# The order of TensorE written into the source, and weights loaded where the first graph needs them: a four-layer graph network

## The chip, the cores and the metric

The kernel runs on one core of one Trainium2 chip, as one launch. The metric is the device time of that launch in microseconds. A core has five engines that run side by side, each with its own instruction queue: TensorE (PE in the profile, its weight loads as PEld), VectorE (DVE), ScalarE (ACT), GpSimd (POOL) and SyncE (SP), which issues the kernel's transfers. They wait for each other through semaphores. Matrix products land in banks of PSUM, all other tiles lie in SBUF.

## The reference

32 graphs, each with 512 nodes of 256 features and a 512 x 512 integer adjacency matrix, go through four layers that all use the same adjacency. After each layer stands a residual sum and a layer norm without parameters.

```python
def reference(x, adj, ...):                      # x: (32, 512, 256), adj: (32, 512, 512)
    # layer 0: four heads of 64; weight by edge type, leaky relu, masked softmax, bias,
    # relu, + h, then a layer norm for each head
    x = _layernorm(x + _L0_gnn_ref(x, adj, W, a_src, a_dst, bias, ln_gamma, ln_beta))
    # layer 1: one head; h = x W, e = relu(f_src + f_dst), masked softmax, att h, elu
    x = _layernorm(x + _L1_gnn_ref(x, adj, W, a))
    # layer 2: transformer block: qkv, eight heads of 32 with the mask
    # adj or adj transposed or the diagonal, Wo, layer norm,
    # feed forward 256 -> 1024 -> 256 with relu, layer norm
    x = _layernorm(x + _L2_gnn_ref(x, adj, Wqkv, bqkv, Wo, bo, ln1, W1, b1, W2, b2, ln2))
    # layer 3: one head; leaky relu (0.2), masked softmax, att h
    x = _layernorm(x + _L3_gnn_ref(x, adj, W, a))
    return x
```

## The kernel before

A graph stays on the chip from its load to its store. All products with 512 nodes are made in blocks of 128 rows (`R` = 4) and 128 features (`K` = 2).

The steps of a graph, with the names under which their tiles stand in the profile:

- *load* and *masks*: `adjt` and `adj` come in halves of 256 rows into one buffer (tag `adj`), SyncE issues them (L320 is the first of them). ScalarE makes `at`, the transposed adjacency in bytes (L340). VectorE makes `a2`, the symmetric mask (`tensor_max`, L347). In the rows of `ADDED`, `a2` is turned into 0 for an edge and -2^127 for none.
- *layer 0*: `h0p` (L297) is x times the weights and eight more columns for the two attention vectors. For each head, `along` transposes one column into a row on all partitions (`gp`, L311; copied by ScalarE to `gb`, L315), VectorE makes the masked numerators `pt` (`kept`, L360), and sixteen products of 65 columns (`o0`, L386; 32 instructions in the profile) fill a bank. After the four heads stand a layer norm for each head (`head_layernorm`) and one over the row (`layernorm`: `bn` and `rs` on VectorE, a power on GpSimd at L243, `y` on ScalarE at L248).
- *layer 1*: transposes `xt1p` (L285), `h1p` (L297), `gp1`, four rows of `o1` (`attend`, L415) with a reciprocal (L440), relu and exp behind each.
- *qkv*: transposes `xt2p`, products `qkp` (L458) and `vp` (L484). q and k are split in a high and a low part (`hi`, `lo`) that 64 transfers on SyncE's queue rearrange into `qk`.
- *attention*: four head pairs. For each block of rows a score product `s` (L506), in the rows of `ADDED` a second product that adds the mask (L514, identity times `a2`), the exponential (L515, ScalarE), and in the other rows a multiplication with the mask (L518, VectorE). Then sixteen instructions `cp` (L526), the product with V.
- *projection*: transposes `ctp` and `ct` (their copies by ScalarE at L277), `wop` (L567).
- *feed forward*: transposes `ytp`, products `f1p` (L590) and `f2p` (L604). The layer norms around it are folded in part into the weights (`bf1p`, L199, and the scaling of `wf1` at L208) and the vectors.
- *layer 3*: like layer 1: `xt3p`, `h3p`, `gp3`, `o3` (L415).

PSUM is split by stage: the steps up to layer 1 take two banks (tag `mma`), qkv to projection four (`mmb`), the rest two (`mmc`).

**What sets the order.** The kernel is written graph by graph, but every step carries a priority, and a list scheduler orders the instructions of each engine by it:

```python
PERIOD = 457
RANK = {"load": 120, "layer 0": -480, "layer 1": -330, "qkv": 0, ...}
    def step(name):
        tc.trace_state.cur_priority = first + PERIOD * b + RANK[name]
```

So four graphs are in work at a time: while graph g is in layers 0 and 1, graph g-1 is in attention, g-2 in projection and feed forward, g-3 in layer 3. Within this the scheduler places instructions one by one. The `cp` products of a head pair are kept together by a raised priority and an added dependency ("one go").

**The weights.** Ahead of the first graph, SyncE issues the loads of all weights and vectors (L123 to L193), among them short columns taken out of vectors with a stride (`bqk`, `bvc`, `bf1`, L134 to L138, and `lnc`, L193), and broadcasts of a vector to all partitions (`bcast`, L94). Then come the set-up computations (L162 to L208): the attention vectors multiplied into columns of the weights (products at L170, reductions at L162 and L176), a bias through `wo` (`bop`) and one through `wf1` (`bf1p`). The first graph's loads are issued after these.

Of the kernel before, what the change touches and what calls it, by code (L numbers as in the profile page):

```python
# [24 lines left out]
ADDED = (1, 3)  # L25
# [3 lines left out]

PERIOD = 457  # L30
RANK = {
    "load": 120,
    "layer 0": -480,
    "layer 1": -330,
    "qkv": 0,
    "attention": 80,
    "projection": 480,
    "feed forward": 510,
    "layer 3": 550,
}  # L40
ALL = mybir.DependencyInfo(mybir.DependencyClass.Sync, mybir.DependencyReason.DATA)
# [22 lines left out]
def fast_path(ctx: ExitStack, tc: tile.TileContext, a: dict, out: bass.AP, bad: bass.AP):  # L64
# [24 lines left out]
    const = ctx.enter_context(tc.tile_pool(name="const", bufs=1))  # L89

    def bcast(src: bass.AP, name: str, n: int, pool=None):

        t = (pool or const).tile([P, n], F32, name=name)
        nc.sync.dma_start(t, bass.AP(tensor=src.tensor, offset=src.offset, ap=[[0, P], [1, n]]))  # L94
        return t
# [19 lines left out]
    def load_w(src: bass.AP, name: str, cols: int, extra: int = 0):  # L115
        kk = src.shape[0] // P
        t = const.tile([P, kk, cols + extra], F32, name=name)
        nc.sync.dma_start(t[:, :, :cols], src.rearrange("(k p) c -> p k c", p=P))
        return t

    w0 = const.tile([P, K, D + 2 * H], F32, name="w0")
    for k in range(K):
        nc.sync.dma_start(  # L123
            w0[:, k, :D].rearrange("p (h e) -> p h e", h=H),
            a["w0"][:, k * P : (k + 1) * P, :].rearrange("h p e -> p h e"),
        )
    w1g = load_w(a["w1g"], "w1g", D, 2)
    w3g = load_w(a["w3gt"], "w3g", D, 2)
    wqkv = load_w(a["wqkvt"], "wqkv", 3 * D)
    wo = load_w(a["wot"], "wo", D)  # L130
    wf1 = load_w(a["w1t"], "wf1", F)
    wf2 = load_w(a["w2t"], "wf2", D)
    bqk = const.tile([P, 2 * K], F32, name="bqk")
    nc.sync.dma_start(bqk, a["bqkv"][: 2 * D].rearrange("(c p) -> p c", p=P))  # L134
    bvc = const.tile([P, K], F32, name="bvc")
    nc.sync.dma_start(bvc, a["bqkv"][2 * D : 3 * D].rearrange("(c p) -> p c", p=P))
    bf1 = const.tile([P, NF], F32, name="bf1")
    nc.sync.dma_start(bf1, a["b1"].rearrange("(c p) -> p c", p=P))  # L138
    bo = bcast(a["bo"], "bo_b", D)
    lnb2 = bcast(a["b2"], "b2_b", D)  # L140
    bias0 = bcast(a["bias0"], "bias0_b", D)
    gam0 = bcast(a["gam0"], "gam0_b", D)
    bet0 = bcast(a["bet0"], "bet0_b", D)
    ln1g = bcast(a["ln1g"], "ln1g_b", D)
    ln2g = bcast(a["ln2g"], "ln2g_b", D)
    ln2b = bcast(a["ln2b"], "ln2b_b", D)

    with (
        tc.tile_pool(name="setup", bufs=1) as setup,
        tc.tile_pool(name="setup_ps", bufs=1, space=bass.MemoryType.PSUM) as setup_ps,  # L150
    ):

        for s, name in enumerate(("a0s", "a0d")):
            ab = setup.tile([P, H, HO], F32, name=name + "_b")
            src = a[name]
            nc.sync.dma_start(
                ab,
                bass.AP(tensor=src.tensor, offset=src.offset, ap=[[0, P], [T * HO, H], [1, HO]]),
            )
            for k in range(K):  # L160
                prod = setup.tile([P, H, HO], F32, name="prod")
                nc.vector.tensor_mul(prod, w0[:, k, :D].rearrange("p (h e) -> p h e", h=H), ab)  # L162
                nc.vector.tensor_reduce(
                    w0[:, k, D + s * H : D + (s + 1) * H], prod, axis=X, op=ALU.add
                )
        for w, name in ((w1g, "a1"), (w3g, "a3")):
            ab = bcast(a[name], name + "_b", 2 * D, setup)
            for s in range(2):
                prod1 = setup.tile([P, K, D], F32, name="prod1")
                nc.vector.tensor_mul(  # L170
                    prod1,
                    w[:, :, :D],
                    ab[:, s * D : (s + 1) * D].unsqueeze(1).to_broadcast([P, K, D]),
                )
                u = setup.tile([P, K], F32, name="u")
                nc.vector.tensor_reduce(u, prod1, axis=X, op=ALU.add)  # L176
                for k in range(K):
                    nc.vector.tensor_copy(w[:, k, D + s : D + s + 1], u[:, k : k + 1])

        p = setup_ps.tile([P, 512], F32, name="bop")  # L180
        for k in range(K):
# [6 lines left out]
            )  # L188
        nc.vector.tensor_add(bo, bo, p[:, :D])

        lnc = setup.tile([P, K, 2], F32, name="lnc")
        for i, name in enumerate(("ln1g", "ln1b")):
            nc.sync.dma_start(lnc[:, :, i], a[name].rearrange("(k p) -> p k", p=P))  # L193
        ln1b = bcast(a["ln1b"], "ln1b_b", D, setup)
        nc.vector.tensor_add(lnb2, lnb2, ln1b)
        p = setup_ps.tile([P, NF, 1], F32, name="bf1p")
        for f in range(NF):
            for k in range(K):
                nc.tensor.matmul(  # L199
                    p[:, f, :],  # L200
# [1116 lines left out]
```

## Time and profile before

| | us |
|---|---|
| time, median of 3 runs (4004.65 to 4009.49) | 4009.25 |
| the profiled execution's own time | 4009.25 |
| its span | 4007.5 |
| TensorE busy (96%) | 3837.6 |
| VectorE busy (63%) | 2509.2 |
| ScalarE busy (50%) | 1986.3 |
| GpSimd busy (8%) | 315.4 |

The span runs from the first instruction to the last. A busy share is the sum of an engine's instructions over the span. The profile names a group by line, engine, operation and tile (output and inputs, without buffer numbers). "L386 ... o<-hv,pt" is the line of layer 0's head products. A wait is listed with the engine that released it. A matrix product with 32-bit inputs shows as two instructions.

### The profile page before, as it was taken

How to read it: one execution, taken by the hardware profiler on the slowest of the kernel's cores; microseconds unless marked ns; L12 is line 12 of the kernel's file. 1: busy time of each engine (PE TensorE's matmuls, PEld its weight loads, DVE VectorE, ACT ScalarE, POOL GpSimd, SP SyncE). 2: the span in 40 equal slices, each digit the busy share in tenths (PEclk: the TensorE clock that was granted, in tenths of full speed). 3: DMA queues.
4: the chain of work that ended last, by engine and by line, in shares of the span. 5: the costliest groups of instructions: out<-in, count | busy, mean ns of one | idle time of the engine just before them, and what ended most of it. 6: DMA issues, size and time to landing. Idle time of an engine off the chain costs nothing.

```text
span 4007.5 us, 53877 instructions
## 1 busy us (share of the span) xinstructions
PE 3837.6 (96%) x19494; PEld 2817.2 (70%) x19494; DVE 2509.2 (63%) x5444; ACT 1986.3 (50%) x4257; POOL 315.4 (8%) x266
## 2 busy tenths in 40 slices
PE   4899999999999999999999999999999999999996
PEld 4567777777777777767777777777777777777654
DVE  4566666676666667666667666667666666666643
ACT  1345555455455455455545555545555545555532
POOL 0000000000000000000000000000000000000000
PEclk7899999999999999999999999999999999999998
DMA  3222222222222222222222122222222222222110
GB/s 106 74 69 56 61 64 64 79 74 59 61 60 64 79 79 59 60 61 65 74 80 69 54 61 66 70 79 69 56 61 63 69 79 69 59 62 65 48 48 12
DMA packets 184367, 261.22 MB, mean 65 GB/s; under 512 B 41120, under 2 KB 76832, under 8 KB 184096
## 3 DMA queue, kind: packets, MB, share of 16 engines
q1 hardware_dynamic: 184096, 257.71, 23.1%
q8 instruction: 157, 2.57, 0.3%
q14 instruction: 114, 0.93, 0.1%
HBM read 106.57 MB, written 16.78 MB: 31 GB/s over the span
## 4 chain that ended last, share of the span: by engine, by line
PE 77%; DVE 12%; ACT 6%; POOL 3%; issue 1%; SPq 0%; DMA 0%; POOLq 0%; ACTq 0%; DVEq 0%
PE f1p L590 11%; PE o L386 11%; PE f2p L604 10%; PE cp L526 9%; PE o L415 6%; PE qkp L458 6%; PE s L506 5%; ACT y L248 3%; PE h1p L297 3%; PE wop L567 3%; PE vp L484 3%; DVE pt L360 3%; POOL rs L243 3%; PE gp L311 2%; PE s L514 2%; DVE bn L239 2%
## 5 line engine op out<-in xcount | busy, mean ns | idle before, releaser
L515 ACT ACTIVATE pr<-s 128x512 f32<-128x512 f32 x1024 | 575.8, 606 | 330.0 <-PE s L514 185.1
L518 DVE TENSOR_TENSOR pr<-pr,a 128x1024 f32<-128x1024 f32 x256 | 309.2, 1217 | 510.1 <-ACT pr L515 510.1
L386 PEld LDWEIGHTS o<-hv,pt 128*128 128x128 f32 x4096 | 542.5, 196 | 67.4 <-DVE pt L360 30.6
L360 DVE SCALAR_TENSOR_TENSOR pt<-gb,ex,at 128x512 f32<-128x512 f32 x768 | 537.1, 742 | 83.7 <-ACT gb L315 83.5
L604 PE MATMUL f2p<-wf,ft 128*128 128x256 f32 x2048 | 575.4, 391 | 6.5 <-ACT ft L599 6.2
L248 ACT ACTIVATE y<-y,rs 128x256 f32<-128x256 f32 x768 | 405.0, 591 | 327.3 <-DVE rs L244 297.2
L590 PE MATMUL f1p<-yt,wf 128*128 128x256 f32 x2048 | 557.0, 381 | 0.5 <-ACT yt L277 0.5
L386 PE MATMUL o<-hv,pt 128*128 128x65 f32 x4096 | 543.4, 273 | 11.9 <-DVE pt L360 11.9
L506 PE MATMUL s<-qk 128*128 128x512 f32 x1024 | 508.4, 538 | 6.8 <-ACT pr L515 4.7
L415 PE MATMUL o<-h,pt 128*128 128x257 f32 x2048 | 503.9, 384 | 8.0 <-DVE pt L360 4.4
L526 PE MATMUL cp<-pr,v 128*64 128x512 f32 x2048 | 470.6, 602 | 3.6 <-ACT pr L515 3.6
L604 PEld LDWEIGHTS f2p<-wf,ft 128*128 128x128 f32 x2048 | 363.9, 191 | 136.3 <-issue 48.7
L415 PEld LDWEIGHTS o<-h,pt 128*128 128x128 f32 x2048 | 379.9, 190 | 111.3 <-issue 29.3
L590 PEld LDWEIGHTS f1p<-yt,wf 128*128 128x128 f32 x2048 | 371.5, 191 | 71.3 <-ACT yt L277 1.1
L243 POOL TENSOR_TENSOR rs<-rs,mhalf 128x4 f32<-128x4 f32 x192 | 216.4, 1127 | 2346.5 <-DVE rs L242 2298.8
L599 ACT ACTIVATE ft<-f1p,bf 128x256 f32<-128x256 f32 x512 | 218.9, 472 | 321.1 <-PE f1p L590 319.4
L526 PEld LDWEIGHTS cp<-pr,v 128*64 128x64 f32 x2048 | 136.6, 137 | 267.4 <-issue 211.1
L239 DVE BATCH_NORM_STATS2 bn<-y 128x6 f32<-128x256 f32 x768 | 296.5, 408 | 1.6
L458 PE MATMUL qkp<-xt,wqkv 128*128 128x512 f32 x512 | 245.1, 608 | 4.2 <-ACT xt L277 4.2
L506 PEld LDWEIGHTS s<-qk 128*128 128x128 f32 x1024 | 192.5, 191 | 70.1 <-issue 23.8
L315 ACT COPY gb<-gp 128x512 f32<-128x512 f32 x192 | 112.3, 585 | 194.9 <-PE gp L311 193.7
L514 PE MATMUL s<-a,identb 128*128 128x512 bf16 x512 | 196.6, 384 | 0.0
(134 smaller groups left out, 4678.7 us busy)
## 6 DMA issues: line engine op xcount, KB each, us to landing
qk<-hi SPq DMA_DIRECT2D x1024, 64.0 KB, 2.0
qk<-lo SPq DMA_DIRECT2D x1024, 64.0 KB, 2.0
adjt<-in_adjt SPq DMA_DIRECT2D x64, 512.0 KB, 3.4
adj<-in_adj SPq DMA_DIRECT2D x64, 512.0 KB, 3.6
xt<-in_xt SPq DMA_DIRECT2D x32, 512.0 KB, 3.4
x<-in_x SPq DMA_DIRECT2D x32, 512.0 KB, 4.6
out<-y SPq DMA_DIRECT2D x32, 512.0 KB, 2.9
wf<-in_w1t SPq DMA_DIRECT2D x1, 1024.0 KB, 9.6
```

The costliest lines, as they stand in the source:

```text
L239: nc.vector.bn_stats(st[:, r, :], y[:, r, :])
L243: nc.gpsimd.tensor_tensor(rs[:, 1, :], rs[:, 0, :], mhalf[:, :R], op=ALU.pow)
L248: nc.scalar.activation(y[:, r, :], y[:, r, :], AF.Identity, bias=rs[:, 2, r : r + 1], scale=rs[:, 1, r : r + 1],)
L360: nc.vector.scalar_tensor_tensor(t, g, f, edges, op0=ALU.max, op1=ALU.mult)
L386: nc.tensor.matmul(o[:, r, :], pt[j][:, r * P : (r + 1) * P], hv[:, j, hh, :], start=j == 0, stop=j == R - 1,)
L415: nc.tensor.matmul(p[:, : D + 1], pt[j][:, r * P : (r + 1) * P], h[:, j, : D + 1], start=j == 0, stop=j == R - 1,)
L458: nc.tensor.matmul(p, wqkv[:, k, (s * K + c) * P : (s * K + c + 1) * P], xt[:, k, :], start=k == 0, stop=k == K - 1,)
L506: nc.tensor.matmul(s, qk[hp][:, 1, i, j * P : (j + 1) * P], qk[hp][:, 0, i, :], start=True, stop=j not in ADDED,)
L515: last = nc.scalar.activation(t[:, i, :], s, AF.Exp, scale=QSCALE)
L526: m = nc.tensor.matmul(cp[i * 2 * DH : (i + 1) * 2 * DH, :], v[:, j, first : first + 2 * DH], pr[j][:, i, :], start=j == 0, stop=j == R - 1,)
L590: nc.tensor.matmul(p[:, f, :], wf1[:, k, (ff + f) * P : (ff + f + 1) * P], yt[:, k, r * P : (r + 2) * P], start=k == 0, stop=k == K - 1,)
L604: nc.tensor.matmul(acc[:, i, :], ft[:, f, i * P : (i + 1) * P], wf2[:, ff + f, :], start=ff + f == 0 and i == 0, stop=ff + f == NF - 1 and ...
```

## The change

TensorE's order is taken from the scheduler and written out. Each step is now a generator that yields before each of its units (the transposes into one bank, one block of rows of a product, one head pair's `cp` and so on), and `PLACES` gives each unit a place on a common scale. Graph b's units stand at `PERIOD * b + place`, and the units of all graphs are merged by that number; within a unit TensorE's instructions stand as written. The other engines' instructions are still ordered by the scheduler. The raised priority and the added dependency of `cp` go.

The loads of the weights, and the computations on them, move into the steps: when graph 0 comes to a step, that step's weights are asked for first. The first layer's weights and vectors reach the chip already joined (`w0t`, `a0`), and the short columns come as one tile `cols` in one transfer. The `bop` and `bf1p` products stand among TensorE's units of graphs 0 and 1.

The rows that take the mask by addition are 2 and 3 instead of 1 and 3. `a2` becomes two tiles, `a2m` for rows 0 and 1 in bytes and `a2a` for rows 2 and 3 in bf16, and one instruction replaces two. `xt0`, the input of layer 0's projection, has a buffer of its own.

```diff
-ADDED = (1, 3)
+ADDED = (2, 3)
...
-PERIOD = 457
-RANK = {
-    "load": 120,
-    "layer 0": -480,
-    "layer 1": -330,
-    "qkv": 0,
-    "attention": 80,
-    "projection": 480,
-    "feed forward": 510,
-    "layer 3": 550,
+PERIOD = 1205
+PLACES = {
+    "edges": [-490],
+    "x": [-197],
+    "layer 0": [
+        2, 11, 56, 83, 172, 302, 302, 302, 302, 302, 405, 405, 405, 405, 435, 533, 545, 545, 545,
+        553, 586, 586, 674, 674,
+    ],
+    "layer 1": [846, 871, 896, 920, 944, 949, 969, 1091, 1117, 1174, 1193],
+    "qkv": [1452, 1452, 1532, 1538, 1567, 1667, 1704, 1704, 1718, 1782],
+    "attention": [
+        1787, 1890, 1909, 1909, 1926, 1926, 1926, 1933, 1988, 1988, 2036, 2071, 2079, 2134, 2167,
+        2209, 2246, 2269, 2294, 2318,
+    ],
+    "projection": [2399, 2404, 2408, 2446, 2496, 2496, 2527, 2581, 2635, 2649],
+    "feed forward": [
+        2859, 2873, 2946, 2977, 2977, 2990, 3026, 3114, 3136, 3166, 3185, 3224, 3250, 3291, 3320,
+        3368, 3426, 3471,
+    ],
+    "layer 3": [3670, 3670, 3679, 3706, 3706, 3711, 3725, 3837, 3837, 3837, 3856],
 }
+STAGES = {"edges": "a", "x": "a", "layer 0": "a", "layer 1": "a", "feed forward": "c", "layer 3": "c"}
...
+    def paced(b, name, units):
+
+        i = 0
+        while True:
+            stage[0] = STAGES.get(name, "b")
+            try:
+                next(units)
+            except StopIteration as end:
+                return end.value
+            yield PERIOD * b + PLACES[name][i]
+            i += 1
...
-    for k in range(K):
-        nc.sync.dma_start(
-            w0[:, k, :D].rearrange("p (h e) -> p h e", h=H),
-            a["w0"][:, k * P : (k + 1) * P, :].rearrange("h p e -> p h e"),
-        )
-    w1g = load_w(a["w1g"], "w1g", D, 2)
-    w3g = load_w(a["w3gt"], "w3g", D, 2)
...
-    bqk = const.tile([P, 2 * K], F32, name="bqk")
-    nc.sync.dma_start(bqk, a["bqkv"][: 2 * D].rearrange("(c p) -> p c", p=P))
-    bvc = const.tile([P, K], F32, name="bvc")
-    nc.sync.dma_start(bvc, a["bqkv"][2 * D : 3 * D].rearrange("(c p) -> p c", p=P))
-    bf1 = const.tile([P, NF], F32, name="bf1")
-    nc.sync.dma_start(bf1, a["b1"].rearrange("(c p) -> p c", p=P))
...
+    cols = const.tile([P, 5 * K + NF], F32, name="cols")
...
+    def weights0():
+        load_w(w0, "w0t")
+        ab = part("a0")
+        bcast(ab, "a0")
+        bcast(bias0, "bias0")
...
+    def weights13(w, name, vectors):
+        load_w(w, name)
+        ab = part(vectors)
+        bcast(ab, vectors)
...
+    def weights2():
+
+
+        load_w(wo, "wot")
+        bcast(bo, "bo")
+        bcast(ln2b, "ln2b")
+        p = bank("bop")
...
+    def weights_ff():
+
+        load_w(wf1, "w1t")
+        load_w(wf2, "w2t")
+        bcast(ln1g, "ln1g")
+        bcast(lnb2, "b2")
+        bcast(ln2g, "ln2g")
+        ln1b = part("ln1b")[:, :D]
+        bcast(ln1b, "ln1b")
...
-        a2 = sb.tile([P, R, N], BF16, tag="a2", name="a2", bufs=2)
+        a2 = [
+            sb.tile([P, R // 2, N], dtype, tag=name, name=name, bufs=2)
+            for dtype, name in ((U8, "a2m"), (BF16, "a2a"))
+        ]
...
-        for r in ADDED:
-            nc.vector.tensor_scalar(
-                a2[:, r, :], a2[:, r, :], 0.0, SHUT, op0=ALU.is_equal, op1=ALU.mult
-            )
+        nc.vector.tensor_scalar(a2[1], a2[1], 0.0, SHUT, op0=ALU.is_equal, op1=ALU.mult)
...
-            gb = along(ex[:, 0, hh, :].unsqueeze(2), "gb0")
+            gb = yield from along(ex[:, 0, hh, :].unsqueeze(2), "gb0")
             pt = [kept("pt0", gb, at[:, j, :], ex[:, 1, hh, j : j + 1]) for j in range(R)]
             p = bank("o0")
             o = p[:, : R * HC].rearrange("p (r c) -> p r c", r=R)
             for r in range(R):
+                yield
...
-                    last = nc.scalar.activation(t[:, i, :], s, AF.Exp, scale=QSCALE)
+                        nc.tensor.matmul(s, identb, a2[1][:, j % 2, :], start=False, stop=True)
+                    nc.scalar.activation(t[:, i, :], s, AF.Exp, scale=QSCALE)
                 if j not in ADDED:
-                    edges = a2[:, j, :].unsqueeze(1).to_broadcast([P, 2, N])
-                    last = nc.vector.tensor_mul(t, t, edges)
+                    edges = a2[0][:, j, :].unsqueeze(1).to_broadcast([P, 2, N])
+                    nc.vector.tensor_mul(t, t, edges)
                 pr.append(t)
 
+            yield
...
+            yield
             cp = bank("cp")
-            with tc.high_priority(offset=4000):
-                for j in range(R):
-                    for i in range(2):
-                        first = (2 * hp + i) * VC
-                        m = nc.tensor.matmul(
-                            cp[i * 2 * DH : (i + 1) * 2 * DH, :],
-                            v[:, j, first : first + 2 * DH],
-                            pr[j][:, i, :],
-                            start=j == 0,
-                            stop=j == R - 1,
-                        )
-                        if j == 0 and i == 0:
-                            tc.add_manual_dep(m.ins, last.ins.name, ALL, reason="one go")
+            for j in range(R):
+                for i in range(2):
+                    first = (2 * hp + i) * VC
...
-    first = tc.trace_state.cur_priority - min(RANK.values())
-
-    def step(name):
-        tc.trace_state.cur_priority = first + PERIOD * b + RANK[name]
-
-    for b in range(B):
...
+    def load_all(b):
+        if b == 0:
+            weights0()
+        at_a2 = masks(b, *load(b))
+        yield
+        return at_a2
...
+    def layer1_all(b, x, at, rd):
+        if b == 0:
+            weights13(w1g, "w1g", "a1")
+        return (yield from layer1(x, at, rd))
...
+    def graph(b):
+        yield PERIOD * b + PLACES["edges"][0]
...
+        at, a2 = yield from paced(b, "edges", load_all(b))
+        xt, x = yield from paced(b, "x", load_x(b))
+        x = yield from paced(b, "layer 0", layer0_all(b, x, xt, at, rds[0]))
...
+        x = yield from paced(b, "layer 3", layer3_all(b, x, at, rds[3]))
...
+    with tc.manual_schedule(engines={mybir.EngineType.PE}):
+        for _ in heapq.merge(*(graph(b) for b in range(B))):
+            pass
```

## The prediction

> **What bounds the kernel now.** I read the page first, for the share of each engine and the forty slices; then the windows by stage, the waits of PE in the steady part, and the chain in order of time through the head and the first graph.
>
> The page:
>
> ```profile
> PE 3837.6 (96%) x19494; PEld 2817.2 (70%) x19494; DVE 2509.2 (63%) x5444; ACT 1986.3 (50%) x4257; POOL 315.4 (8%) x266
> PE   4899999999999999999999999999999999999996
> PEclk7899999999999999999999999999999999999998
> ```
>
> TensorE is busy for 96% of the span, and every slice but the first two and the last is full. The windows (columns: length, busy time of each engine, granted clock, DMA share, GB/s):
>
> ```profile
> 0.00:44.00 44.00, 9.06 (x36) 8.08 (x36) 11.78 (x30) 0.00 (x0) 2.76 (x10) 1.00 0.53 153
> 44.00:87.00 43.00, 36.55 (x160) 33.50 (x160) 19.98 (x36) 11.46 (x23) 0.00 (x0) 0.63 0.20 67
> 87.00:104.00 17.00, 0.05 (x1) 0.05 (x1) 11.67 (x21) 4.46 (x10) 3.93 (x2) 0.50 0.30 93
> 128.00:280.00 152.00, 135.58 (x687) 92.65 (x688) 93.39 (x163) 63.45 (x134) 9.37 (x6) 0.93 0.26 67
> 400.00:3590.00 3190.00, 3151.08 (x16217) 2319.31 (x16216) 2074.94 (x4524) 1656.83 (x3556) 261.04 (x214) 1.00 0.24 66
> 3925.00:4007.50 82.50, 52.11 (x198) 38.86 (x198) 21.49 (x57) 18.27 (x42) 3.02 (x3) 0.81 0.04 14
> ```
>
> From 400 to 3590, TensorE idles 39 of 3190 us, 1.2%, at full clock. A graph takes 119.5 us there (a head pair's product with V starts at 1003.74 and again at 1123.26). So an order can give at most 1.5 us a graph, unless it does worse. The rest lies in the first 280 us and in the last 80. PE's waits between 400 and 3590, the three largest (total, times, longest, us):
>
> ```profile
> PE wop L567 <- ACT ct L277: 13.7, 27, 0.5
> PE xt3p L285 <- ACT y L248: 11.6, 27, 0.4
> PE o L386 <- DVE pt L360: 6.6, 27, 0.2
> ```
>
> The chain through the head and graph 0 (start, length, what):
>
> ```profile
> 6.73 5.05 SPq L136
> 12.74 3.08 SPq L94
> 17.29 5.72 DMA bet_b<-in_bet
> 23.46 5.95 DMA lnc<-in_ln1b
> 29.45 7.00 PE bf1p L199 x32
> 40.61 4.78 DMA adjt<-in_adjt
> 55.67 13.30 PE o L386 x60
> 103.30 0.61 ACT y L248
> ```
>
> SyncE issues all weights one after another, the set-up of L199 to L208 follows the last, and only then does graph 0's load (L320) go out. The first projection (h0p) starts at 44.42. Then head outputs in a row, then a layer norm with TensorE empty from 86.1 to 103.95.
>
> **The change part by part.** The profiled execution's own time is 4009.25 (span 4007.5 and 1.75 around it), which is also the median of the runs shown.
>
> *Head.* Graph 0's step now asks first for w0, the a0 vectors and bias0, then adjt, xt and x; everything else comes behind. The first h0p needs w0 with its reduced columns. The a0 broadcast goes out second, at 1.25 (row of the second issue of L123), and the 256 KB a_b row lands in 7.0; two products of 0.69 (L170) and four small reductions of 0.42 (L162) follow: 1.25 + 7.0 + 1.38 + 1.68 = 11.3. That is 33.1 less than 44.42. Bounds from the head's own landings: 3.2 (b_b) makes it 36.9, 11.8 (w2t) makes it 28.3. I take 7.0 as the same size and shape. The first half of adjt and xt are asked for by about 4 (half a microsecond an issue, L118) and land 4.0 and 3.9 after issue in the head's rows, by 8: hidden. So is the second half of adjt, if it waits only for its buffer: the first is read by 11 (1.28 and 1.15, L340), a load of 4.8 and two more copies end by 18.5, and the first pt comes at about 19.
>
> *Graph 0's layer 0.* Before, TensorE sees the edge row of the next head (gp, L311) among the head outputs. In the new order gp of head h+1 stands behind all sixteen o0 of head h, so three heads run in series: gp 0.87, gap 0.2, its copy gb 0.59 (L315), gap 0.1, four masked rows pt 2.73 (0.76 each less overlap with the matmuls, L360), gap 0.1, and the last 26 of the matmuls that still follow, at 13.30/60 = 0.222 each, 5.76. Sum 10.35, against (86.06 - 54.35)/4 = 7.9 now. Three times 2.4: +7.3.
>
> The granted clock in that stretch bears on this:
>
> ```profile
> 55.00:110.00 55.00, 27.68 (x126) 27.09 (x126) 0.51 0.21 68
> ```
>
> That row is L386 alone: 13.30 us of unbroken 65-column matmuls and still half clock, so I take half clock for the heads after the change as well.
>
> The Trainium skill (TensorE: Matmul & The Clock Gate, Part 1) says otherwise: the gate opens after about 3.4 us of sustained activity and shuts after an idle window of that length. By the page the unbroken o0 would have run at full speed, and a head of graph 0 would take about 7.5 us, an estimate from that page, with a sum lower by some 11 us. The page also speaks against this change: it puts gaps of about 4 us into graph 0, where TensorE waits for gb and pt, and each would shut the gate. The row disagrees with the first and cannot show the second.
>
> *Work put between.* Weights of layer 1 are prepared on VectorE when graph 0 comes to layer 1, and graph 1's masks come in as well, both into the queue of graph 0's layer norm, whose chain is bare (87 to 104): two tensor_max of 1.205 (L347), two products 0.69, one reduction 0.68: +4.5. Bounds 0, and 7.9 with four products and four reductions.
>
> *bop and bf1p.* The 32 single-column matmuls (7.00, L199) and bop (2.08) leave the head, where the DMA queue would now hide them, and stand in TensorE's order in graphs 0 and 1. At full clock half of 9.08, and a share 135.58/152 = 0.89 of the time there is TensorE's: +4.0. Bounds 0 and 9.1.
>
> Head to 280 us: -33.1 + 7.3 + 4.5 + 4.0 = -17.3.
>
> *Steady part.* The order of units is nearly the present one, but whole units now stand together. Between the last ct transpose and wop stand 3.0 us of TensorE's work instead of none; between f2p and xt3p 16.5 instead of 15.2; between an edge row gp of layer 0 and its o0 at least 5.2 instead of 2.2 (each the sum of the trace's durations of what lies between). These exceed what has to be hidden (ACT's ct copy 0.5 late, y 0.4 late, pt 0.2 late), so the three waits go: 13.7/27 + 11.6/27 + 6.6/27 = 1.18 a graph. What is next: gp3 now follows the last h3p at once, where 0.66 of other work stood. The copy h (0.36), the small exp (0.21) and semaphores make 0.70, bare. I take 0.66; bounds 0 and 1.0. The three last o1 of layer 1 stand behind the last product with V of the attention (before, nine of its sixteen matmuls came first), and then h0p of the next graph takes the same two banks of stage "a": a wait for rd, relu and exp of o1 (0.59 each, L248's kind). The nearest row is the idle time before o1 and o3 now (o L415, 8.0 over 32 graphs): 0.25 a graph, a third of it, 0.08, for the last three o1. The far end is 1.9, the rival below. I take 0.3, near the row. So -1.18 + 0.66 + 0.3 = -0.22, for 29 graphs (280 to 3740 at 119.5): -6.4.
>
> Taking the mask additively in rows 2 and 3 instead of 1 and 3, one SHUT instruction instead of two and the split mask tile: equal counts on TensorE, less than 0.1 us on VectorE, which has 37% free. Nothing. If that cover went, it would be 0.1 a graph.
>
> SyncE: fewer issues in the head, none moved past a steady copy; its queue carries the same 64 copies a graph. The late weights all go out within its first 33 issues, ahead of the first of those copies. Nothing.
>
> *Drain.* The last two wop units stand behind three o3 of graph 30, work that TensorE has to do anyhow, but the last feed forward then starts later: +1 (0 to 5.2, the three o3: 24 instructions at 0.216 from start to start).
>
> Sum: 4009.25 - 17.3 - 6.4 + 1 = 3986.6.
>
> **The rivals.**
> (A) The waits go and nothing new comes. Head and graph 0 as above, -17.3; steady -1.18 x 29 = -34.2: 4009.25 - 17.3 - 34.2 + 1 = 3959. For it: covers of 3 to 16 us are all larger than the chains they hide. Against: bare h3p to gp3.
> (B) Slower: VectorE becomes late at o1. The window behind the last head pair:
>
> ```profile
> 1040.80:1070.90 30.10, 28.91 (x148) 23.28 (x148) 24.47 (x70) 16.43 (x41) 2.02 (x2) 1.00 0.10 36
> ```
>
> VectorE is busy for 81% of it. It works through ln2g, the sum with x and the next bn of the feed forward, and the reciprocal of o1 (L440), at 1045.36, comes 4.5 us after the product with V has ended. The new order wants that bank again 3.5 us after, and the relu and exp take 0.84 more: 4.5 + 0.84 - 3.5 = 1.9 of wait a graph. In place of my 0.3 this is -1.18 + 0.66 + 1.9 = +1.4 a graph, x 29 = +40: 4009.25 - 17.3 + 40 + 1 = 4033. It decides from 16.3/29 = 0.56 net loss a graph on, and it is slower by over 0.2% from 0.84 on. For it: today the scheduler can move TensorE to another ready unit; a fixed order waits for the engine that is late. Against: today this lateness costs almost nothing, 8.0 in all at o L415.
> (C) The change does not do what it says: the weights still queue in front (w1g and wqkv go out ahead of the second adjt half, whose buffer must be read first), the norm of graph 0 stretches, and steady waits are only exchanged. At its bounds the head then gives 28.3 - 7.3 - 7.9 - 9.1 = 4, so 4006 with the drain; steady -0.2 to +0.35 a graph (x 29: -6 to +10) makes it 4001 to 4017, taken as no change.
>
> **How the numbers follow.** Forecast 0.38 at 3987; (A) 0.25; (B) 0.27; (C) 0.10. The forecast's own bounds: up by gp3 at 1.0 (+10), the landing at 11.8 (+5) and the drain (+4), 4006; down by gp3 at 0 and the turn at 0.08 (-0.88 x 29 = -25), which is all but (A). The low end 3950 is (A) less 3.8 (landing at 3.2) and 4.0 (bf1p hidden). The high end 4030 cuts off the upper half of (B), 0.14, and a little of (A) falls below. A measurement of this kernel can tell about 0.2%, 8 us. Forecast and (A) are faster by more: 0.63; (C) is within: 0.10; (B) slower: 0.27.
>
> **What would show it.** In the profile after: the first h0p at 11 (9.5 to 16); gaps of about 4 us between the o0 of graph 0's heads, at clock 0.5 in 20 to 65; xt1p of graph 0 about 25 us earlier than 103.95. The waits wop on ct and xt3p on y gone, and one new of gp3 on h3's exp, 0.6 to 0.7 times some 30. The distance between rows of the same head pair's product with V 119.3. I am wrong if that distance is 120.3 or more (then look whether TensorE waits at o1 or h0p, for rd or relu and exp), if the window 400 to 3590 shows more than 39 us idle, or if the first h0p comes after 30.

## The result, and the profile after

The changed kernel takes 3972.68 us (median of four runs, 3970.98 to 3974.81) against 4009.37 before (four runs beside it): ratio 0.9911, 95% interval 0.9894 to 0.9928. Its profiled execution took 3970.98, 38.3 less than the one of before (4009.25); the span fell from 4007.5 to 3969.2. The forecast was 3987.

The page of the changed kernel:

```profile
span 3969.2 us, 53826 instructions
PE 3806.5 (96%) x19367; PEld 2824.3 (71%) x19494; DVE 2523.9 (64%) x5402; ACT 1959.5 (49%) x4257; POOL 294.5 (7%) x266
```

The weight loads (PEld) are as many as before, 19494; of the products 127 have no record, nearly all of them the identity products that add the mask, four a graph. Where they are missing the trace shows short gaps that were none (4.6 us in all between 400 and 3590), so I go by starts instead. The period, here and below, is the mean distance of the first product with V of graphs 5 to 25: 119.52 before, 118.60 after. In the chain two such rows lie 118.62 apart:

```profile
3616.26 3.63 PE cp L547 x16
3734.88 3.63 PE cp L547 x16
```

The head and graph 0, from TensorE's timeline (start, length, line, tiles, and in brackets the idle time before and its releaser):

```profile
10.71 5.54 PE L318 MATMUL h0p<-w,xt 128*128 128x264 f32 x16 [10.71 <-DMA xt<-in_xt]
30.18 7.71 PE L403 MATMUL o<-hv,pt 128*128 128x65 f32 x32 [1.55 <-DVE pt L376]
40.34 7.70 PE L403 MATMUL o<-hv,pt 128*128 128x65 f32 x32 [1.60 <-DVE pt L376]
50.49 7.71 PE L403 MATMUL o<-hv,pt 128*128 128x65 f32 x32 [1.60 <-DVE pt L376]
79.38 2.81 PE L305 MATMUL xt1p<-ident,y 128*128 128x128 f32 x8 [21.18 <-ACT y L267]
```

The first projection starts at 10.7 (44.4 before). The heads now come one every 10.15 us, each behind a pause, and the layer norm leaves TensorE empty for 21.2 instead of 17.9. The windows by stage (columns as before: length, busy time of each engine, clock, DMA share, GB/s):

```profile
10.50:79.00 68.50, 39.19 (x160) 34.61 (x160) 36.18 (x64) 13.11 (x28) 3.93 (x2) 0.58 0.43 144
79.00:272.00 193.00, 174.67 (x810) 125.49 (x815) 105.51 (x193) 77.41 (x165) 11.05 (x8) 0.87 0.23 61
400.00:3590.00 3190.00, 3138.83 (x16256) 2339.40 (x16362) 2105.97 (x4516) 1645.59 (x3582) 242.34 (x215) 1.00 0.24 67
```

The second is the one to look at: from 79 to 272 the clock is 0.87, where before the same length from its own first xt1p on (104 to 297) had 0.93. PE's waits between 400 and 3590 (total, times, longest):

```profile
PE gp L333 <- ACT ex L648: 19.0, 27, 0.7
PE o L433 <- ACT exp L460: 13.0, 27, 0.5
PE h0p L318 <- ACT exp L460: 9.0, 27, 0.3
PE h3p L318 <- ACT h L325: 5.6, 27, 0.2
```

The three waits of before (wop, xt3p, o of layer 0: 31.9 in all) are gone. In their place stand 46.6 us of others. Yet a graph is 0.92 shorter. That is what the experiments had to explain.

How the 38 us come about, by the same event in both traces (weight-load starts):

| event | before | after | difference |
|---|---|---|---|
| first h0p | 44.4 | 10.7 | -33.7 |
| first xt1p of graph 0 | 104.0 | 79.4 | -24.6 |
| last cp of graph 1 | 320.1 | 307.6 | -12.5 |
| last cp of graph 30 | 3786.1 | 3747.3 | -38.7 |
| TensorE's end | 3999.1 | 3961.0 | -38.0 |

The head gains 33.7, graphs 0 and 1 give 21 of it back, the 29 graphs between gain 26, and the drain costs 0.7.

### The profile page after: what moved, and what is told of

It reads as the page before. It is cut to its first block, busy times and chain, and to the rows that moved or that the text cites. A ratio compares the mean times of both kernels' runs of the same rounds, so it can differ in the third digit from the quotient of the medians.

```text
span 3969.2 us, 53826 instructions
## 1 busy us (share of the span) xinstructions
PE 3806.5 (96%) x19367; PEld 2824.3 (71%) x19494; DVE 2523.9 (64%) x5402; ACT 1959.5 (49%) x4257; POOL 294.5 (7%) x266
## 4 chain that ended last, share of the span: by engine, by line
PE 50%; DVE 17%; ACT 12%; issue 9%; POOL 5%; POOLq 0%; DVEq 0%; ACTq 0%
PE o L403 10%; ACT y L267 6%; PE f2p L627 6%; PE f1p L612 6%; PE o L433 6%; PE qkp L477 5%; POOL rs L262 3%; PE cp L547 3%; DVE pr L539 3%; PE h1p L318 3%; PE vp L504 3%; PE wop L588 3%; DVE bn L258 2%; POOL st L289 2%; PE gp L333 2%
## 5 line engine op out<-in xcount | busy, mean ns | idle before, releaser
L536 ACT ACTIVATE pr<-s 128x512 f32<-128x512 f32 x1024 | 546.3, 605 | 160.2 <-PE s L527 93.3
L403 PEld LDWEIGHTS o<-hv,pt 128*128 128x128 f32 x4096 | 506.4, 199 | 34.4 <-issue 20.2
L403 PE MATMUL o<-hv,pt 128*128 128x65 f32 x4096 | 503.3, 280 | 8.1 <-DVE pt L376 8.1
L627 PE MATMUL f2p<-wf,ft 128*128 128x256 f32 x2048 | 491.3, 383 | 10.6 <-ACT ft L621 5.3
L612 PE MATMUL f1p<-yt,wf 128*128 128x256 f32 x2048 | 488.7, 381 | 2.6 <-ACT yt L296 2.6
L539 DVE TENSOR_TENSOR pr<-pr,a2m 128x1024 f32<-128x1024 f32 x256 | 309.8, 1221 | 253.2 <-ACT pr L536 253.1
L527 PE MATMUL s<-qk 128*128 128x512 f32 x1024 | 450.4, 519 | 3.0 <-DMA qk<-lo 1.7
L621 ACT ACTIVATE ft<-f1p,cols 128x256 f32<-128x256 f32 x512 | 214.8, 471 | 401.6 <-PE f1p L612 401.6
L262 POOL TENSOR_TENSOR rs<-rs,mhalf 128x4 f32<-128x4 f32 x192 | 194.5, 1013 | 1904.7 <-DVE rs L261 1831.2
L411 DVE RECIPROCAL rd<-o 128x4 f32<-128x4 f32 x128 | 23.1, 181 | 270.9 <-PE o L403 270.9
```

The costliest lines, as they stand in the source:

```text
L403: nc.tensor.matmul(o[:, r, :], pt[j][:, r * P : (r + 1) * P], hv[:, j, hh, :], start=j == 0, stop=j == R - 1,)
L527: nc.tensor.matmul(s, qk[hp][:, 1, i, j * P : (j + 1) * P], qk[hp][:, 0, i, :], start=True, stop=j not in ADDED,)
L536: nc.scalar.activation(t[:, i, :], s, AF.Exp, scale=QSCALE)
L539: nc.vector.tensor_mul(t, t, edges)
L612: nc.tensor.matmul(p[:, f, :], wf1[:, k, (ff + f) * P : (ff + f + 1) * P], yt[:, k, r * P : (r + 2) * P], start=k == 0, stop=k == K - 1,)
L627: nc.tensor.matmul(acc[:, i, :], ft[:, f, i * P : (i + 1) * P], wf2[:, ff + f, :], start=ff + f == 0 and i == 0, stop=ff + f == NF - 1 and ...
```

## The experiments

Three theories for the steady gain. **S**: fewer changes of kind on TensorE, from one kind of product to another (172 a steady graph in the built order before and 72 after; counted along the products of the traces 182 and 91). **W**: single waits that the places avoid. **M**: the rows that take the mask by addition. Each run below was timed beside runs of the kernel before, whose median in the three groups was 4012.5 to 4013.1 (4009.4 beside the changed kernel). In the code shown, lines are left out at `...`, and remarks behind # are explanations.

| kernel | median us | ratio to before, interval | first h0p | period |
|---|---|---|---|---|
| before | 4009.4 | | 44.4 | 119.52 |
| changed | 3972.7 | 0.9911 [0.9894, 0.9928] | 10.7 | 118.60 |
| undo_order | 4231.5 | 1.0558 [1.0531, 1.0586] | 15.4 | 127.5, unsteady |
| weights_first | 3984.8 | 0.9927 [0.9910, 0.9944] | 29.6 | 118.62 |
| halves | 4610.7 | 1.1489 [1.1470, 1.1508] | 10.5 | 139.4 |
| rows_1_3 | 4001.3 | 0.9968 [0.9957, 0.9980] | 11.0 | 119.49 |
| undo_order_rows | 4005.3 | 0.9983 [0.9973, 0.9993] | 16.4 | 119.52 |
| gp3_later | 4104.7 | 1.0223 [1.0206, 1.0240] | 10.0 | 123.4 |
| ctp_between | 3976.7 | 0.9906 [0.9890, 0.9923] | 11.0 | 118.43 |
| halves_few | 4207.5 | 1.0484 [1.0466, 1.0501] | 10.5 | 126.3 |
| alternate | 3977.1 | 0.9910 [0.9894, 0.9927] | 10.6 | 118.75 |
| fill_two | 3966.7 | 0.9887 [0.9870, 0.9903] | 10.7 | 118.60 |
| fill_warm | 3970.6 | 0.9896 [0.9880, 0.9913] | 10.5 | 118.58 |
| fill_ctp | 3963.7 | 0.9879 [0.9863, 0.9896] | 10.4 | 118.43 |

### One part of the change at a time

undo_order (`paced` sets the priorities of before, and `cp` has the raised priority and "one go" again):

```diff
-    with tc.manual_schedule(engines={mybir.EngineType.PE}):
-        for _ in heapq.merge(*(graph(b) for b in range(B))):
+    first = [tc.trace_state.cur_priority - min(RANK.values())]
+    for b in range(B):
+        for _ in graph(b):
             pass
```

> The changed kernel, but TensorE's order is again left to the scheduler with the priorities and the raised cp of before; weights stay late. All theories: the first h0p stays near 10.7 us. Theory S (the steady gain of 0.92 us a graph comes from fewer changes of kind on TensorE, 182 to 91 a graph at 16 ns): the built order has 167 changes of kind a graph against 172 before and 72 after, so the period goes back to 119.4 to 119.6 and the time to 3985 to 3998. Rival W (the gain comes from single waits that the places avoid): the same period, since this order gives the waits back; the run tells only how much belongs to the order (12 to 25 us) and how much to the weights (11 to 24 us). Rival M (the mask rows or the late weights make the steady gain): the period stays at 118.6 and the time near 3973.

Measured: none of the three; 4231 us, and an unsteady period, 126.4 in most graphs and up to 135.3 in some. With as many changes of kind as before, the built order is another one (all of wop behind o3, for one). Its largest wait:

```profile
PE s L539 <- DVE lo L500: 53.3, 25, 2.1
```

So this run could not be read as "the order undone", and the next two were made to part it.

weights_first:

```diff
     with tc.manual_schedule(engines={mybir.EngineType.PE}):
+        weights0()
+        bcast(bet0, "bet0")
+        bcast(gam0, "gam0")
+        weights13(w1g, "w1g", "a1")
...
+        weights_ff()
+        weights13(w3g, "w3gt", "a3")
```

> The changed kernel with its fixed order, but all weights are loaded and prepared ahead of the first graph's loads. Theories S and W: the period stays at 118.6, bf1p and bop leave graphs 0 and 1, the first h0p comes at 35 to 44 instead of 10.7, and the half-clock stretch behind bf1p in graph 1 goes; time 3972.7 + 24 to 33 for the head - 4 to 12 for the rest: 3985 to 4000. If the order of the queue hardly matters (the change does not do what it says): within 5 us of 3973.

Measured 3984.8, period 118.62, at the lower edge of the 3985 to 4000 expected: the late loads are worth nothing in the period, and 12 us in the first graphs (graph 30's last cp is at 3759.5 against 3747.3; the intervals of the two ratios overlap, since the runs of before beside them differ by 4 us). The first h0p came at 29.6, earlier than expected (35 to 44); that the joined loads make a shorter queue in front of it is likely, but not shown. So of 18.9 us at the first h0p 12.2 remain.

rows_1_3:

```diff
-ADDED = (2, 3)
+ADDED = (1, 3)
...
-                rows = a[name][b, h * N // 2 : (h + 1) * N // 2]
-                nc.sync.dma_start(t, rows.rearrange("(r p) j -> p r j", p=P))
+                rows = a[name][b].rearrange("(r h p) j -> h p r j", h=2, p=P)[h]
+                nc.sync.dma_start(t, rows)
```

> The changed kernel, but rows 1 and 3 take the mask by addition, as before (the halves of the adjacency are loaded as rows 0, 2 and 1, 3, so that the mask stays in two tiles). Theories S and W: the period stays within 0.15 of 118.6, time 3969 to 3977. Rival M (the choice of rows matters, since two added rows in a row let ScalarE run on without VectorE just ahead of the product with V): the period is 0.3 or more longer, time 3981 or more.

Measured 4001.3: rival M. The rows, which the prediction had costed at nothing, are worth 23 us (by the two ratios) to 29 us (by the two times) in the fixed order. The period's median is 119.36 against 118.59. The wait that grows is that of o1 (waits of PE in this kernel, 13.0 in the changed one):

```profile
PE o L433 <- ACT exp L460: 32.8, 27, 1.2
```

Why, is seen on VectorE's timeline around the last head pair of a graph. The changed kernel (the cp there starts at 1375.36), then this one (1387.00):

```profile
1370.40 2.35 DVE L539 TENSOR_TENSOR pr<-pr,a2m 128x1024 f32<-128x1024 f32 x2
1373.39 0.75 DVE L258 BATCH_NORM_STATS2 bn<-y 128x6 f32<-128x256 f32 x2
1374.39 0.17 DVE L261 SCALAR_TENSOR_TENSOR rs<-mv 128x4 f32<-128x4 f32 x1
```

```profile
1382.41 1.22 DVE L539 TENSOR_TENSOR pr<-pr,a2m 128x1024 f32<-128x1024 f32 x1
1384.71 0.75 DVE L258 BATCH_NORM_STATS2 bn<-y 128x6 f32<-128x256 f32 x2
1385.46 1.19 DVE L539 TENSOR_TENSOR pr<-pr,a2m 128x1024 f32<-128x1024 f32 x1
1386.78 0.16 DVE L261 SCALAR_TENSOR_TENSOR rs<-mv 128x4 f32<-128x4 f32 x1
```

With rows 2 and 3 added, both mask products (L539) are done before the feed forward's layer norm comes. With rows 1 and 3, the product of row 2 falls into the middle of it. The norm's rs then stands 0.22 before cp instead of 0.97, and what follows it is as much later: the four y on ScalarE, then on VectorE two products and the next norm's statistics, and behind these in VectorE's queue the reciprocal rd of o1. The changed kernel, then this one:

```profile
1382.11 0.14 DVE L458 RECIPROCAL rd<-o 128x1 f32<-128x1 f32 x1
```

```profile
1394.48 0.14 DVE L458 RECIPROCAL rd<-o 128x1 f32<-128x1 f32 x1
1394.65 0.47 ACT L459 ACTIVATE relu<-o,rd 128x256 f32<-128x256 f32 x1 [3.07 <-DVE rd L458]
```

Counted from cp, rd and with it o1's relu and exp come 0.73 later than in the changed kernel. TensorE waits for the bank that exp reads, and that wait is longer by the same 0.73 a graph (19.8 over 27).

undo_order_rows: the edits of undo_order and of rows_1_3 together. The built order of a steady graph is that of before.

> The changed kernel with TensorE's order left to the scheduler and rows 1 and 3 taking the mask by addition, both as before; the weights stay late. The built order of a steady graph is instruction for instruction that of before. This is the change of the weights alone. Theory: period 119.5, first h0p near 11, and the head's gain kept better than in the changed kernel, since the scheduler puts the edge rows early in graph 0: 12 to 28 us less than before, time 3982 to 4000. Theory S2 (the rows matter only through the order): the jump to 126 of the last run with the scheduler was the rows', so it is gone here. Rival (late weights disturb the scheduler): period 124 or more, time above 4150.

Measured 4005.3, period 119.52. So the rows 2 and 3 had ruined the scheduler's order, and the late weights by themselves (with the split mask tile and xt0's own buffer, which stay) gain only 0.17% (interval 0.07 to 0.27%), although the first h0p comes 28 us earlier than before. That is less than the least expected (12). At the first cp of graph 1 the lead was 9.2 us, at that of graph 2 it was gone, and TensorE's end is 1.3 earlier than before (all in the profiled executions). From its first h0p to graph 3's first cp, this kernel has 116 us at half clock and 60 us of idle TensorE; before has 75 and 47, the changed kernel 109 and 52.

### Changes of kind

halves and halves_few: neighbouring units of different stages done in halves, in turn (halves_few: only o0 beside xt2p, qkp and vp).

```diff
+            if half:
+                yield None          # in paced: half of a unit is done
+                continue
...
+                    if j == 1:
+                        yield True  # in layer 0's o0, and so in the other units
...
-        for _ in heapq.merge(*(graph(b) for b in range(B))):
-            pass
+            if heap and stages.get(heap[0][1], "a") != stages[b]:
+                _, c = heapq.heappop(heap)
+                done = run(c)       # half of c behind half of b
+                run(b)
```

> The changed kernel, but where two neighbouring units belong to steps of different stages, TensorE does half of one, half of the other, and then the two second halves. The work, the weights and the places are the same; changes of kind in the built order rise from 72 to 169 a graph. Theory S (16 ns for each change): 97 x 0.016 = 1.55, period about 120.1, time about 4018. Rival W (only waits count): period 118.6 plus what new waits the page shows, 118.4 to 119.0, time 3967 to 3985.

> The changed kernel, but only neighbours of layer 0 and qkv (o0 beside xt2p, qkp, vp) are done in halves, in turn: 90 changes of kind a graph in the built order against 72. Theory S (16 ns for each change of kind): +0.29, period 118.9. Rival (changes of kind cost nothing by themselves): 118.5 to 118.7 unless a new wait shows.

Measured 4611 and 4208, far beyond either theory: the halves moved units together that need a distance. In halves, f2p now stands half a unit behind the f1p it needs:

```profile
PE f2p L648 <- ACT ft L642: 150.1, 69, 5.2
```

In halves_few, layer 0's o0 waits for pt, and the clock is no longer full in the steady part (window 400 to 3590):

```profile
400.00:3590.00 3190.00, 3073.55 (x15249) 2285.61 (x15348) 1990.04 (x4227) 1547.23 (x3364) 231.42 (x203) 0.96 0.23 63
```

Neither tells S from W. They tell how narrow the order is.

alternate: only xt1p and h1p beside f1p and f2p, one product of each in turn, little else displaced.

```diff
+        pair = {"layer 1", "feed forward"}
...
+            if not done and heap and {stages.get(heap[0][1]), stages[b]} == pair:
```

> The changed kernel, but where a unit of layer 1 and one of feed forward are neighbours (xt1p, h1p beside f1p, f2p), TensorE does one product of each in turn: 87 changes of kind a graph in the built order against 72, with little else displaced. Theory S (a change of kind costs 16 to 29 ns by itself): +0.24 to +0.43, period 118.84 to 119.03. Rival (it costs nothing there; what the fixed order saved was short waits and turns of banks, and the products with the mask): 118.50 to 118.70.

Measured 118.75: +0.15 for 15 changes, between both. The waits are those of the changed kernel to within 0.1 us, in total. If the 0.15 is all due to the changes, one costs about 10 ns here, not 16 to 29.

### The waits that the new order has

gp3_later:

```diff
-    "projection": [2399, 2404, 2408, 2446, 2496, 2496, 2527, 2581, 2635, 2649],
+    "projection": [2399, 2404, 2408, 2446, 2496, 2496, 2504, 2510, 2525, 2649],
```

> The changed kernel with four other places: wop's first three units stand before h3p's last, behind it, and behind gp3, so that gp3 no longer follows the last h3p at once. If gp3's bare wait (19.0 us in 27 graphs, 0.70 each) and h3p's (0.2) are what the fixed order costs here: period 117.7 to 117.9, time 3943 to 3953. Rival (the time comes back as a wait of wop for ct or of o3 for pt): 118.3 to 118.7.

Measured 4104.7, period 123.4. The waits of gp3 and h3p did go; the rival's kind of wait came, in another place, and with it a price that neither theory had:

```profile
PE o L403 <- DVE pt L376: 50.7, 26, 2.3
```

```profile
1219.20:1229.40 10.20, 10.20 (x38) 8.53 (x39) 6.13 (x12) 1.17 (x2) 0.00 (x0) 0.50 0.36 88
```

The first line is of the waits, the second a window of the same kernel. The wait is for the fourth pt of the second head, and VectorE's queue shows why it is late:

```profile
1214.28 2.08 DVE L376 SCALAR_TENSOR_TENSOR pt<-gb,ex,at 128x512 f32<-128x512 f32 x3 [0.40 <-ACT gb L337]
1217.24 1.23 DVE L366 TENSOR_TENSOR a2a<-at,adj 128x1024 bf16<-128x1024 uint8 x1 [0.89 <-DMA adj<-in_adj]
1218.38 0.75 DVE L376 SCALAR_TENSOR_TENSOR pt<-gb,ex,at 128x512 f32<-128x512 f32 x1
```

VectorE's order is still the scheduler's. With the new places it put the next graph's mask a2a ahead of that last pt, in all 26 graphs between 400 and 3590, and there the mask waits for its load of adj. In the changed kernel a2a stands behind the pt. So the run does not tell what gp3's and h3p's 0.9 are worth by themselves.

The pause came amid 65-column products, and the clock fell to half behind it for 3.4 to 10.2 us in 21 of the 26 graphs. In the five graphs where it did not, the period is 120.5 to 120.8, in those with 10.2 us of half clock 125.4 to 125.5. So of the 4.8 that the period grew about 2.0 comes without any half clock (by the list, 1.95 of this wait and 0.55 of o3 for pt came, gp3's and h3p's 0.9 went), and the rest goes with it.

ctp_between:

```diff
-    "projection": [2399, 2404, 2408, 2446, 2496, 2496, 2527, 2581, 2635, 2649],
+    "projection": [2355, 2390, 2404, 2446, 2496, 2496, 2527, 2581, 2635, 2649],
```

> The changed kernel with two other places: the first two ctp units stand between the last three o1 units instead of behind them. If o1's wait for relu and exp (0.48 a graph) and h0p's (0.33) are bank turns that other work of TensorE can cover: period 117.8 to 118.1, time 3945 to 3958. Rival (VectorE is late anyway, and the reciprocals and products behind ctp now stand in its queue ahead of o1's): 118.5 or more, time 3970 or more.

Measured 118.43, 3976.7, the rival by the time and between the two by the period. The waits of o1 (13.0) and h3p (5.6) are gone, but h0p's has grown by slightly more than both (9.0 before this edit):

```profile
PE h0p L318 <- ACT exp L460: 28.8, 27, 1.1
```

The wait was passed on. The period's 0.17 a graph, 5 us, was lost again ahead of graph 3, whose first cp is 9.9 later: half clock up to there rose from 109 to 123 us.

### Graphs 0 and 1

fill_two:

```diff
+                if ahead and r == 0 and hh + 1 < H:       # graph 0 only
+                    pts[hh + 1] = yield from rows(hh + 1)
...
             weights13(w1g, "w1g", "a1")
+            nc.sync.dma_start(cols, a["cols"])
+            weights2()
+            weights_ff()
```

> The changed kernel with two edits to graph 0: the next head's edge row (gp) stands behind the first quarter of each head's o0, and bop and bf1p stand ahead of xt1p, in the time of graph 0's layer norm in which TensorE is empty. Theory (the head's gain was given back to heads in series, to bf1p and to the half clock behind it): heads of graph 0 32 us instead of 38, no half clock behind bf1p in graph 1; period 118.6; time 10 to 16 less than the changed kernel, 3957 to 3964. Rival (whatever graph 0 gains, graph 1 waits out, since its masks and copies are what is late): 3968 to 3975.

Measured 3966.7, between theory and rival; graph 30's last cp is 8.0 earlier than in the changed kernel (3739.3 against 3747.3), where 10 to 16 were expected. The heads took 30.5 instead of 38.2, as expected, but xt1p stayed at 79.7. On VectorE's timeline, inside graph 0's layer norm:

```profile
60.44 0.17 DVE L225 TENSOR_TENSOR cols<-cols,bf1p 128x8 f32<-128x8 f32 x1 [5.07 <-PE bf1p L218]
```

The sum that takes bf1p stands in VectorE's queue ahead of the norm's next step and waits 5.07 for TensorE: the heads' gain went there. What did come is the other half: bf1p and the half clock behind it left graph 1 (its first cp is 7.9 earlier, 255.5 instead of 263.4).

fill_warm, the edits of fill_two and, behind graph 0's last o0:

```diff
+            p = bank("warm")
+            for i in range(30):
+                nc.tensor.matmul(
+                    p, ident, v.rearrange("p r c -> p (r c)")[:, :512], start=True, stop=True
+                )
```

> The kernel of the two edits to graph 0, with 30 products of 512 columns more that nobody reads, put into TensorE's empty time behind graph 0's last o0. It computes the same outputs. Theory (the half clock after the empty time is what makes xt1p and h1p of graph 0 slow, 8.5 us in the changed kernel): clock 1.0 there, xt1p and h1p 4.5 to 5.5, and 2 to 6 less than with the two edits alone. Rival (the extra products delay xt1p, or the granted clock does not answer to them): the same time or more.

Measured 3970.6: the rival, for the first of its reasons and not quite the second. Its timeline and its windows:

```profile
51.44 27.94 PE L699 MATMUL warm<-v,ident 128*128 128x512 f32 x60
80.07 4.42 PE L218 MATMUL bf1p<-cols,wf 128*128 128x1 f32 x32
```

```profile
51.40:55.40 4.00, 4.00 (x7) 1.82 (x7) 3.55 (x6) 0.00 (x0) 0.00 (x0) 0.50 0.04 14
55.50:82.50 27.00, 27.00 (x83) 13.64 (x81) 15.12 (x31) 4.37 (x8) 3.93 (x2) 1.00 0.20 64
82.70:89.50 6.80, 6.80 (x25) 5.64 (x26) 2.18 (x4) 0.96 (x2) 0.00 (x0) 0.50 0.00 0
```

The clock does answer: full 4 us after the wide products begin. But they end late (xt1p at 84.4), and bf1p, 32 products of one column, takes the clock down again within 3 us, so that xt1p and most of h1p run at half after all.

fill_ctp: the edits of fill_two and ctp_between together.

> The two edits to graph 0 together with the two ctp units between the last o1. Theory (a period of 118.42 stays, and the 8 us that the ctp edit lost before graph 2 were half clock around bop and bf1p, which now stand elsewhere): 5 less than with the two edits alone, 3951 to 3959. Rival (the ctp edit's loss in the first graphs stays): 3962 to 3970.

Measured 3963.7, the lowest of all here, and the rival (3962 to 3970): period 118.43, and 3 less than fill_two instead of 5; at graph 3's first cp it is still 3.4 behind fill_two (496.5 against 493.1). The two intervals overlap, so which of these two is better is not settled; both lie below the changed kernel's range.

## Why the prediction came out as it did

The time lay 14 us below the forecast and inside the range, on the side that was forecast; by terms:

| term | predicted | measured |
|---|---|---|
| first h0p | -33.1 | -33.7 |
| heads of graph 0 in series, half clock | +7.3 | +6.5 |
| weights and masks in the norm | +4.5 | +3.3 |
| bop, bf1p and the rest up to graph 1's last cp | +4.0 | +12.1 |
| steady part | -6.4 | -26.2 |
| drain | +1 | +0.7 |

The measured column is missing 0.7, a shorter way from the first h0p to the first o0.

The distance between the same products with V is 118.60, where 119.3 was forecast. That the sum came within 14 us is in part luck, since two misses of opposite sign stand in it: 8 too little for bop and bf1p, 20 too little gain in the steady part.

*The head: the size right, the step not.* It came out within 0.6 us, but by luck. The chain that the prediction named, the a0 broadcast and the reductions of w0, was done at 7.8 and not at 11.3:

```profile
6.41 1.39 DVE L170 TENSOR_REDUCE w<-prod 128x4 f32<-128x256 f32 x4
```

What the first h0p waited for was xt, which the prediction had landed by 8 and called hidden; it released h0p at 10.7.

*Right.* The heads of graph 0 ran in series, one every 10.15 where 10.35 was worked out, and at half clock (the row of L403 alone):

```profile
20.00:58.00 38.00, 30.23 (x128) 28.05 (x128) 0.51 0.42 140
```

The rule of the Trainium skill that the prediction weighed (TensorE: Matmul & The Clock Gate, Part 1) would have had these at full speed, after 3.4 us of activity; the measurement decides, 38 us at 0.51, and in fill_two 38.1 us at 0.50 without a gap. In the layer norm VectorE does carry the strangers that were named, one tensor_max of 1.22 and a product and a reduction of 0.68 each ahead of the norm's first statistics, more behind:

```profile
69.29 1.22 DVE L366 TENSOR_TENSOR a2m<-at,adj 128x1024 uint8<-128x1024 uint8 x1
71.56 0.68 DVE L183 TENSOR_TENSOR prod<-w1g,a 128x512 f32<-128x512 f32 x1
73.30 0.68 DVE L186 TENSOR_REDUCE w1g<-prod 128x2 f32<-128x512 f32 x1
```

In the steady part the three waits went (-1.18), and gp3's bare wait came at 0.70 where 0.66 was taken.

*Mis-sized: bop and bf1p.* They were priced at their halved durations. But bf1p does not only take 3.6 us at full clock; the clock falls behind it (window of the changed kernel):

```profile
219.00:229.50 10.50, 10.50 (x38) 8.25 (x38) 5.02 (x15) 0.85 (x2) 1.01 (x1) 0.51 0.01 2
```

Taking both products out of graph 1 was worth 7.9 us there (fill_two). In the rest there is half clock too: between the first xt1p and graph 1's last cp TensorE is busy at half clock for 50.3 us instead of 24.2, which is 13 us of work lost, and in fill_two still for 39.4. No run takes this remainder out, so what causes it stays open.

*Mis-sized: the turn of the banks at o1.* It was taken as 0.3 a graph and is 0.81 (13.0 and 9.0 over 27). The slower rival's mechanism, VectorE late at o1 with the reciprocal behind the next norm's statistics, was there (rows_1_3): with the old rows it is 1.55 (32.8 and 9.1 over 27), near the rival's 1.9. The rows that were called worth nothing are what kept most of it away.

*Wrong: "Nothing" for the rows.* Rows 2 and 3 take 0.73 a graph from just that wait, and 0.76 from the median period. The step had looked at TensorE's counts and VectorE's mean load; what counts is where in VectorE's queue the last mask product stands.

*Missing: a price for the order by itself.* The listed waits add up to +0.54 a graph (-1.18, 0.70, 0.81, 0.21 for h3p), the period fell by 0.92, so 1.46 came from elsewhere. The same sum for rows_1_3 gives 1.5 (period's median). At the 10 ns a change that alternate showed, 100 changes less make 1.0. That is carried over from 15 changes between few kinds, and was not tested for the others. The remaining half a microsecond is open. Gaps too short for the list of waits can be only a part of it: they are 0.26 a graph before in all, and not more than 0.17 after.

This is also why two readings of the prediction failed. It took TensorE's idle time, 1.5 us a graph, for all that an order can give; but most of the 1.46 came from stretches in which TensorE counts as busy. And it called itself wrong if the window from 400 to 3590 showed more than 39 us idle. The window shows 51.2, 46.6 without the gaps of missing records, so this sign came true while the period fell: idle time alone did not tell whether the order was better. Without the new rows the period fell by 0.15 (median), near the 0.22 forecast, but as the sum of +1.37 of waits and -1.5 that had no price.

So the forecast's sign rested on the head, as argued, but two thirds of the measured gain are steady. The order and the rows do that only together: periods of 119.49 for the order without the rows, 127.5 for the rows without the order, 119.52 for neither and 118.60 for both. And the head's gain was mostly given back by the filling of the pipeline: of 18.9 us 12.2 remained in the fixed order (weights_first against the changed kernel), of 28 us about 7 or less in the scheduler's (undo_order_rows).

## What to carry to other kernels

Where an order is frozen, price each wait in the place where it lands: the instruction of another engine that stands in its queue just ahead of what TensorE waits for can decide, whatever that engine's mean load. Where only one engine's order is frozen, look at the other queues after every move: the scheduler may have put something new in front (gp3_later). A gain at the very start is only worth what the filling of the pipeline lets through, so measure it at the first steady period and not at the first product. Do not put products of one or few columns, or a pause among them, where the work behind them is long: the price is the half clock that follows.

## What the runs showed of the hardware that was not expected

In these traces the granted clock goes with how many columns the products stream, and not with whether TensorE is busy. In fill_two TensorE works for 38.1 us without a gap, nearly all of it on 65-column and one-column products, and the clock stays at half:

```profile
22.20:60.30 38.10, 38.10 (x174) 37.42 (x174) 17.98 (x32) 6.03 (x11) 0.00 (x0) 0.50 0.44 141
```

In fill_warm one-column products that filled TensorE for 4.4 us took the clock from 1.0 to 0.5, and 512-column products raised it within 4 us. No run varied the columns alone, so another property that narrow products share is not ruled out.

In a steady graph of the changed kernel the 65-column products run at full clock, with wide products between them. With the same products in the same order there, a pause of about 2 us was enough to put the clock at half for 3.4 to 10.2 us in 21 of 26 graphs (gp3_later); in halves_few, where the order differs too, it is 3.4 to 13.7 us in every graph. So a small delay there is multiplied.
